# Row maxima of an attention kernel: one shared 120-row stack against own 64-row stacks, two heads side by side in TensorE

## The chip, the cores and the metric

One core of one Trainium2 chip runs the whole kernel. The metric is the device time of one execution in microseconds (us), the median of several runs. Engines are named as the profile names them: PE is TensorE's matmuls and PEld its weight loads, DVE is VectorE, ACT is ScalarE, POOL is GpSimd, SP is SyncE, which issues most DMAs.

## The reference

A transformer block on x of shape 8 x 1024 x 256: attention with 16 heads of 16, a gated relative position bias, then a layer norm, then a mixture of 8 experts (top 2, with a capacity and a fallback) and a second layer norm. The part that the change touches is the softmax:

```python
q, k, v = split_heads(x @ Wq.T + bq), ...            # 8 x 16 x 1024 x 16
gate_out = gate_a * (gate_b * gru_const - 1.0) + 2.0  # one per batch, head, query
gated_bias = gate_out * pos_bias[None]                # pos_bias depends on key - query
scores = einsum('bhid,bhjd->bhij', q, k) / sqrt(16) + gated_bias
attn = softmax(scores, axis=-1)
```

The bias differs from key to key only near the diagonal; beyond 192 positions it is one constant for each side.

## The kernel before

**Two passes over the scores.** The exponentials are computed with keys in the partitions and queries along the row, so a row's maximum can't be subtracted there. A first pass, "the maxima", therefore computes scores with queries in the partitions, takes the maximum of each row, and stores it, negated, as two more rows of the stacked queries (`shift`). The second pass (`scores`, `exps`) then gets shifted scores out of its matmul.

**Stacks.** q and k are split into three bf16 parts each. A float product is approximated by six products of parts (`PRODUCTS`), and these are stacked in the contraction dimension: 6 x 16 = 96 rows, 24 rows for the constant far bias, 2 for the shift. `QS` and `KS` hold these 122 rows for the two heads of a unit; `KD` holds the same stack (120 rows) for the differences of keys. `load_unit` (L901) fills the stacks of a unit by DMAs from DRAM, 16 rows of each head at a time, all on SyncE's queue.

**The maxima.** The 128 keys of a block are taken as two halves of 64. max(first, second) = second + relu(first - second), so one bank gets the difference of the halves (a=1, keys from `KD`) and one the second half (a=0, from `KS`). Each is one "far" matmul of the 120-row stack with 512 columns (L1023) and one "near" matmul that adds the bias by a diagonal of gates, `dgb` (L1027, `half_scores`). `max_first` (L1037) does a=1 into bank pm1 and lets ScalarE write relu of it to `over`; `max_second` (L1054) does a=0 into pm0, or into the bank that is shared by the other work; `max_fold` (L1060) lets VectorE add both and take the maximum in the next step.

**Order of the work.** The order is written out by hand and each engine runs its list in that order. A unit is two heads of a batch: 64 units of 16 steps. Step s of unit u does one block of keys j and one half c of the queries: `scores` (L1102, two matmuls), `exps` (L1115: VectorE adds the near bias, ScalarE takes exp), and every second step (c=1) `products` with v (L1132: eight matmuls in 32-column parts of the array). In the same step the maxima of step m = g + 21 are done, so they run 21 steps ahead (`LEAD`), one head at a time. Projections, gates, output projection and routing of neighbouring batches are "streams" that are fed in between, at most one bank task a step (`streams.bank`); `held` lets the reader of the bank run in the next step.

**PSUM.** Two score tiles of two banks each, pm0 and pm1, one bank for everything else, one for the products.

**SyncE's list within a unit.** The sums of the outputs (s=2, after ScalarE has copied the products), the loads of `KS`, `KD` (s=3, 4), the sums' return (s=5), `QS` (s=6) of unit u+2, the bias of u+1 (s=8), its gates (s=9 and 15), the divided outputs and the row maxima (s=11, 12).

The lead and the loop over steps:

```python
for m in range(LEAD):
    if m:
        max_fold(m - 1)
    ...
    streams.held()
    max_first(m)
    streams.free()
    streams.bank()
    max_second(m)
```

After attention the mixture of experts runs from about 2490 us to the end; the change doesn't touch it.

Of the kernel before, what the change touches and what calls it, by code (L numbers as in the profile page):

```python
# [21 lines left out]
P = 128  # L22
# [18 lines left out]

PRODUCTS = ((0, 0), (0, 1), (0, 2), (1, 0), (1, 1), (2, 0))
R_FAR, R_SHIFT, R_ALL = 6 * D, 6 * D + 24, 6 * D + 26
HP = 2
LEAD = 21
SHIFT_AT = -LEAD % 16
DIVIDE_AT = 10
EPS = 1e-5

# [29 lines left out]
def tile_attention_moe(  # L79
# [73 lines left out]
    with ExitStack() as at:  # L153
# [210 lines left out]
        for t in fd:  # L364
# [3 lines left out]
            nc.sync.dma_start(  # L368
                out=flat, in_=zero16.unsqueeze(1).to_broadcast([P, flat.shape[1], 2 * E])
            )  # L370
        QS = [cst.tile([R_ALL, HP, N], BF16, name=f"qs{i}") for i in range(3)]
        KS = [cst.tile([R_ALL, HP, N], BF16, name=f"ks{i}") for i in range(3)]
        KD = [cst.tile([R_SHIFT, HP, N // 2], BF16, name=f"ks_d{i}") for i in range(2)]
        pattern = once.tile([R_ALL, HP, N], F32, tag="oD", name="pattern")
        for h in range(HP):
            for part in range(3):
                r = R_FAR + part * NI
                nc.sync.dma_start(out=pattern[r : r + NI, h, :], in_=kcr[:NI, :])
            for r in range(R_SHIFT, R_ALL):
                nc.sync.dma_start(out=pattern[r : r + 1, h, :], in_=kcr[8:9, :])  # L380
        for t in KS:
            nc.gpsimd.tensor_copy(t[R_FAR:], pattern[R_FAR:])
        for t in KD:
            nc.gpsimd.memset(t[R_FAR:], 0.0)
        incl = [cst.tile([P, NE + 1, NI], F32, name=f"incl{i}") for i in range(2)]
        prefix = [cst.tile([P, 2 * NI], F32, name=f"prefix{i}") for i in range(3)]
        for t in prefix:
# [513 lines left out]
        def load_unit(u, which):  # L901

            b, hp = divmod(u, UB)
            assert batches[b].gated and batches[b].rows >= (hp + 1) * HP * D
            heads = slice(hp * HP * D, (hp + 1) * HP * D)
            if which == 2:
                nc.sync.dma_start(
                    out=QS[u % 3][R_FAR:R_SHIFT],
                    in_=fd[b % 2][:, :, hp * HP : (hp + 1) * HP, :].rearrange(
                        "a j h n -> (a j) h n"  # L910
                    ),
                )
            src, dst = ((kd, KS[u % 3]), (dd, KD[u % 2]), (qd, QS[u % 3]))[which]
            for r, parts in enumerate(PRODUCTS):
                nc.sync.dma_start(
                    out=dst[r * D : (r + 1) * D],
                    in_=src[b % 2][parts[which != 2], heads, :].rearrange(
                        "(h d) n -> d h n", d=D
                    ),
                )  # L920

        def load_max_bias(u):

# [86 lines left out]

        def half_scores(m, a, pm):
            u, n = divmod(m, STEPS)
            i, h = divmod(n, HP)
            me = units[u]
            lo, hi = max(i - NEAR, 0), min(i + NEAR + 1, NI)
            pm = pm.rearrange("p (j n) -> p j n", n=HALF)
            if a:
                keys = KD[u % 2][:, h, :].rearrange("p (j n) -> p j n", n=HALF)  # L1020
            else:
                keys = KS[u % 3][:R_SHIFT, h, :].rearrange("p (j n) -> p j n", n=P)[:, :, HALF:]
            nc.tensor.matmul(  # L1023
                pm, QS[u % 3][:R_SHIFT, h, i * P : (i + 1) * P], keys, start=True, stop=False
            )
            at = (h * 2 + a) * MWIN + (lo - i + NEAR) * P
            nc.tensor.matmul(  # L1027
                pm[:, lo:hi, :],
                dgb[m - h][:, h, :],
                me.biasb[:, at : at + (hi - lo) * P].rearrange("p (j n) -> p j n", n=P)[  # L1030
                    :, :, :HALF
                ],
                start=False,
                stop=True,
            )

        def max_first(m):  # L1037

            u, n = divmod(m, STEPS)
            me = units[u]  # L1040
            ahead = m + 6
            if m == 0:
                for a in range(0, 6, 2):
                    dgb[a] = diagonal(0, a // 2)
            if ahead % 2 == 0 and ahead < UNITS * STEPS:
                dgb[ahead] = diagonal(ahead // STEPS, ahead % STEPS // HP)
            if n == 0:
                me.mh = rt.tile([P, HP, NI], F32, tag="mh", name=f"mh{u}", bufs=2)
            me.over = rt.tile([P, CH], F32, tag="over", name="over", bufs=2)
            pm = ps_m.tile([P, CH], F32, tag="pm1", name="pm1")  # L1050
            half_scores(m, 1, pm)
            nc.scalar.activation(me.over, pm, AF.Relu)  # L1052

        def max_second(m, common=False):  # L1054

            pm = bank("pm") if common else ps_m.tile([P, CH], F32, tag="pm0", name="pm0")
            half_scores(m, 0, pm)
            units[m // STEPS].rest = pm

        def max_fold(m):  # L1060
            u, n = divmod(m, STEPS)
            i, h = divmod(n, HP)
            me = units[u]
            nc.vector.tensor_tensor_reduce(  # L1064
                out=me.over,
                in0=me.rest,
                in1=me.over,
                scale=1.0,
                scalar=-3.0e38,
                op0=ALU.add,  # L1070
                op1=ALU.max,
                accum_out=me.mh[:, h, i : i + 1],
            )

        def shift(u):
            me = units[u]
            pmr = bank("pmr")
            nc.tensor.transpose(
                pmr[: HP * NI, :P], me.mh.rearrange("p h i -> p (h i)"), ident
            )  # L1080
            yield HELD
            rows = rt.tile([HP * NI, 2, P], BF16, tag="row", name=f"row{u}", bufs=2)
            nc.scalar.mul(rows[:, 0, :], pmr[: HP * NI, :P], -1.0)
            yield SLOW
            nc.vector.scalar_tensor_tensor(
                rows[:, 1, :], pmr[: HP * NI, :P], -1.0, rows[:, 0, :],
                ALU.mult, ALU.subtract,
            )

            def store():  # L1090
                for a in range(2):
                    nc.sync.dma_start(
                        out=QS[u % 3][R_SHIFT + a : R_SHIFT + a + 1].rearrange(
                            "o h (i q) -> o (h i) q", q=P
                        ),
                        in_=rows[:, a, :],
                    )

            after(1, store)


        def scores(u, j, c):  # L1102
            me = units[u]
            qs, ks = QS[u % 3], KS[u % 3]
            me.sc = ps_s.tile([P, HP, CH], F32, tag="sc", name=f"sc{u}_{j}")
            for h in range(HP):
                nc.tensor.matmul(  # L1107
                    me.sc[:, h, :],
                    ks[:, h, j * P : (j + 1) * P],
                    qs[:, h, c * CH : (c + 1) * CH],  # L1110
                    start=True,
                    stop=True,
                )
# [148 lines left out]
            streams.step()  # L1262
        clear = clearing()
        for u in range(2):
            for which in range(3):
                load_unit(u, which)
            load_max_bias(u)
            clear_max_bias(u)
# [3 lines left out]
        for m in range(LEAD):  # L1272
            if m:
                max_fold(m - 1)
            if m == STEPS:
                streams.drain()
                streams.own.append(shift(0))
            streams.held()
            max_first(m)
            streams.free()  # L1280
            streams.bank()
            max_second(m)
        streams.drain()
        for j in range(2):
            gate_biases(0, j)
# [23 lines left out]
        for g in range(G + 12):  # L1309
# [4 lines left out]
            if g < G:  # L1314
# [5 lines left out]
                if sb == 60:  # L1320
                    streams.start(rows(b))
                if u + 2 < UNITS:
                    for which, at_ in enumerate((3, 4, 6)):
                        if s == at_:
                            load_unit(u + 2, which)
                    if s == 1:
# [1 line left out]
                    if s == 7:  # L1328
                        clear_max_bias(u + 2)
                if u + 1 < UNITS:  # L1330
                    if s == 8:
                        load_bias(u + 1)
                    for which, at_ in enumerate((9, 15)):
# [4 lines left out]
            streams.held()  # L1338
            if g < G:
                scores(u, j, c)  # L1340
                if m < G:
                    max_first(m)
                exps(u, j, c)
            streams.free(c == 1)
            if c == 1 and 1 < g < G + NCH:
                pu, pj = (u, j - 1) if j else (u - 1, NI - 1)
                products(pu, pj, prs)
            if c == 1 and g < G:
                prs = units[u].pr
            if u and s == DIVIDE_AT:  # L1350
                streams.own.append(divide(u - 1))
            if s == SHIFT_AT and u + 1 < UNITS:
# [1 line left out]

            behind = c == 0 and streams.read == SLOW
            others = s + 1 != SHIFT_AT
            if not behind:
                streams.bank(others)
            if m < G and g < G:
                max_second(m, c == 0 and not behind and not streams.holder)  # L1360
            if behind:
                streams.bank(others)
            if g < G and c == 0:
                gu, gj = divmod(g // 2 + 2, NI)
                if gu < UNITS:
# [270 lines left out]
```

## Time and profile before

| | |
|---|---|
| median of 3 runs | 3673.83 us (3670.74 to 3685.23) |
| the profiled execution | 3676.38 us, span 3674.6 us |
| granted TensorE clock, mean | 0.961 |
| PE busy | 3285.5 us, 89% |
| DVE, ACT, POOL busy | 1930.6, 2045.6, 2223.5 us |
| far matmuls, a=1 and a=0 (L1023) | 392.9 and 396.1 us, 1024 each |
| near matmuls (L1027) | 577.9 us, 2048 |
| scores (L1107), products (L1137) | 619.3 us (2048), 553.9 us (4096) |
| exp (ACT L1129) | 1047.4 us, 1024 |

In a row of the profile's groups the first number after the bar is the busy time in us, the next the mean length of one in ns; behind the second bar stands the engine's idle time just before, and what ended most of it. Matmuls overlap: one with 512 columns is shown as 0.38 us long, while the next can start 0.22 us after it. In the timeline a row has its start, its length, the engine, line and operation, the tiles, and in brackets the idle time before it with the releaser. "x8" are eight merged into one row.

### The profile page before, as it was taken

What the parts mean: (1) busy time and instruction counts of PE and PEld (TensorE: products, weight loads), DVE (VectorE), ACT (ScalarE), POOL (GpSimd) and SP (SyncE); (2) the same over time, 40 slices, a digit from 0 to 9 for tenths busy, and PEclk for the clock granted to TensorE, in tenths of its full rate; (3) what the DMA queues carried; (4) which work ended last, traced back from release to release, by engine and by line L of the source; (5) the groups of instructions that cost most, each with busy time, mean ns of one, the idle gap of its engine ahead of it and who ended that gap; (6) DMA issues with size and microseconds to landing.
All of it is one profiled execution on the core that took longest, in us unless ns stands there. A gap on an engine that the chain in (4) does not pass through costs nothing. (4 is left out here: it accounts for less than half of the span.)

```text
span 3674.6 us, 53450 instructions
## 1 busy us (share of the span) xinstructions
PE 3285.5 (89%) x16263; PEld 1656.9 (45%) x16263; DVE 1930.6 (53%) x5559; ACT 2045.6 (56%) x3084; POOL 2223.5 (61%) x2619
## 2 busy tenths in 40 slices
PE   4698999989999999999999999984399999999998
PEld 2243343333334334334334433332267677667776
DVE  2455656655665665665666576651134344444443
ACT  1577777767777777777787777871022222222222
POOL 2566666876887887787787788782233333333332
PEclk8899999999999999999999999996699999999999
DMA  5567666656553444444434444330332322223220
GB/s 130 150 169 200 171 182 182 186 172 185 169 154 112 150 140 128 126 136 126 141 121 148 129 135 130 123 102 14 110 86 59 88 89 56 91 93 94 73 90 21
DMA packets 380593, 455.70 MB, mean 124 GB/s; under 512 B 87653, under 2 KB 285410, under 8 KB 380282
## 3 DMA queue, kind: packets, MB, share of 16 engines
q1 hardware_dynamic: 338602, 388.06, 35.6%
q0 software_dynamic: 19296, 43.38, 4.2%
q10 hardware_dynamic: 22384, 20.58, 1.9%
q8 instruction: 138, 2.26, 0.3%
q14 instruction: 173, 1.42, 0.1%
HBM read 315.16 MB, written 140.54 MB: 124 GB/s over the span
## 5 line engine op out<-in xcount | busy, mean ns | idle before, releaser
L1129 ACT ACTIVATE pr<-sc 128x1024 f32<-128x1024 f32 x1024 | 1047.4, 1024 | 332.2 <-DVE sc L1122 328.8
L983 POOL TENSOR_TENSOR gb<-bias,gates 128x1024 f32<-128x1024 f32 (+2 forms) x512 | 1071.5, 2093 | 178.0 <-DMA gates<-gd 102.6
L1064 DVE CUSTOM_DVE_ANT_0 over<-pm,over 128x512 f32<-128x512 f32 x1024 | 703.7, 687 | 815.0 <-ACT over L1052 302.4
L1052 ACT ACTIVATE over<-pm 128x512 f32<-128x512 f32 x1024 | 611.3, 597 | 280.4 <-PE pm L1027 264.6
L1107 PE MATMUL sc<-qs,ks 122*128 122x512 bf16 x2048 | 619.3, 383 | 42.8 <-ACT pr L1129 32.5
L1122 DVE TENSOR_TENSOR sc<-sc,gb 128x640 f32<-128x640 f32 (+3 forms) x768 | 599.7, 781 | 94.2 <-POOL gb L983 80.9
L1027 PE MATMUL pm<-biasb,dgb 128*128 128x320 bf16 (+2 forms) x2048 | 577.9, 282 | 16.7 <-POOL dgb L996 16.7
L1137 PE MATMUL o_acc<-pr,v 128*17 128x512 f32 x4096 | 553.9, 612 | 0.3 <-ACT pr L1129 0.3
L1474 PE MATMUL ph<-xsT,w 128*128 128x512 f32 (+1 forms) x1440 | 488.6, 497 | 13.0 <-ACT xsT L1414 13.0
L1489 PE MATMUL py<-w,hT 128*128 128x256 f32 x2208 | 485.0, 379 | 6.5 <-DVE ys L1496 6.5
L1489 PEld LDWEIGHTS py<-w,hT 128*128 128x128 f32 x2208 | 419.2, 190 | 75.2 <-issue 9.8
L1023 PE MATMUL pm<-ks,qs 120*128 120x512 bf16 x1024 | 396.1, 387 | 43.8 <-DVE mh L1064 25.1
L1023 PEld LDWEIGHTS <-qs 120*128 120x128 bf16 x2048 | 207.3, 101 | 502.6 <-issue 334.7
L1023 PE MATMUL pm<-ks_d,qs 120*128 120x512 bf16 x1024 | 392.9, 384 | 39.2 <-DMA qs<-qd 25.7
L1481 ACT ACTIVATE hT<-ph,b_sb 128x512 f32<-128x512 f32 (+1 forms) x360 | 211.6, 588 | 288.3 <-PE ph L1474 284.7
L1474 PEld LDWEIGHTS ph<-xsT,w 128*128 128x128 f32 x1440 | 270.7, 190 | 213.3 <-issue 167.3
L1414 ACT COPY xsT<-pt 128x512 f32<-128x512 f32 (+1 forms) x90 | 39.5, 489 | 568.6 <-PE pt L1411 473.8
L143 POOL TENSOR_TENSOR rs<-rstd,neghalf 128x1 f32<-128x1 f32 x138 | 78.3, 567 | 438.4 <-DVE rstd L141 437.5
L1027 PEld LDWEIGHTS <-dgb 128*128 128x128 bf16 x2048 | 201.7, 98 | 278.9 <-issue 147.5
L996 POOL TENSOR_TENSOR dgb<-anti,grev 128x256 bf16<-128x256 f32 x512 | 315.1, 616 | 4.9
L1107 PEld LDWEIGHTS <-ks 122*128 122x128 bf16 x2048 | 197.9, 99 | 227.8 <-issue 82.6
L1509 POOL DMA_INDIRECT out_dram<-o,dst_i x138 | 145.3, 1053 | 158.1 <-DVE o L145 69.5
(184 smaller groups left out, 2861.2 us busy)
## 6 DMA issues: line engine op xcount, KB each, us to landing
gates<-gd SPq DMA_DIRECT2D x64, 832.0 KB
biasb<-stripb SPq DMA_DIRECT2D x128, 288.0 KB
gates<-gd SPq DMA_DIRECT2D x64, 576.0 KB
bias<-blocks SPq DMA_DIRECT2D x64, 512.0 KB
xd<-zero SPq DMA_DIRECT2D x51, 522.0 KB
ks<-kd SPq DMA_DIRECT2D x384, 64.0 KB
qs<-qd SPq DMA_DIRECT2D x384, 64.0 KB
yd<-zero SPq DMA_DIRECT2D x40, 512.0 KB
```

The costliest lines, as they stand in the source:

```text
L983: nc.gpsimd.tensor_tensor(gb_[:, :, off : off + hi - lo], me.bias[:, :, off : off + hi - lo], gates[:, :, lo - at : hi - at], ALU.mult,)
L996: nc.gpsimd.tensor_tensor(dg, anti.unsqueeze(1).to_broadcast([P, HP, P]), batches[b].grev[:, i, hp * HP : (hp + 1) * HP] .unsqueeze(2) .to ...
L1023: nc.tensor.matmul(pm, QS[u % 3][:R_SHIFT, h, i * P : (i + 1) * P], keys, start=True, stop=False)
L1027: nc.tensor.matmul(pm[:, lo:hi, :], dgb[m - h][:, h, :], me.biasb[:, at : at + (hi - lo) * P].rearrange("p (j n) -> p j n", n=P)[:, :, :HALF],
L1052: nc.scalar.activation(me.over, pm, AF.Relu)
L1064: nc.vector.tensor_tensor_reduce(out=me.over, in0=me.rest, in1=me.over, scale=1.0, scalar=-3.0e38, op0=ALU.add, op1=ALU.max, accum_out=me. ...
L1107: nc.tensor.matmul(me.sc[:, h, :], ks[:, h, j * P : (j + 1) * P], qs[:, h, c * CH : (c + 1) * CH], start=True, stop=True,)
L1122: nc.vector.tensor_tensor(sc[:, :, lo - c * CH : hi - c * CH], sc[:, :, lo - c * CH : hi - c * CH], me.gb[j][:, :, off : off + hi - lo], A ...
L1129: nc.scalar.activation(pr, sc, AF.Exp)
L1137: nc.tensor.matmul(o_acc[r : r + D + 1, :], batches[b].v[:, j, hp * HP + h, :], prs[c][:, h, :], start=(j == 0), stop=(j == NI - 1),)
L1474: nc.tensor.matmul(ph[:, :size], w1_sb[:, k, f * P : (f + 1) * P], xsT[:, k, :size], start=(k == 0), stop=(k == NK - 1),)
L1489: nc.tensor.matmul(py, hT[:, f, t * P : (t + 1) * P], w2_sb[:, f, :], start=(f == 0), stop=(f == NF - 1),)
```

## The change

The maxima get stacks of their own. `QM` and `KM` hold, for each head, 64 rows: three products of parts (`M_PRODUCTS`: q0k0, q0k1, q1k0) of 16 rows each, and 16 rows of the far bias in two parts. Head 0 lies in partitions 0 to 63, head 1 in 64 to 127. A step's far matmuls are now those of both heads for one a, each over its 64 rows of the array, into pm0 and pm1; an even step does a=1, the odd one a=0. Thus a pair of steps does what two steps did before. The two Relus come together in the even step, the two folds together at the start of the next even step. `KM` also gets the second halves of the keys as a copy of its own, so that `KS` and `QS` are needed only by the exponentials: two buffers, loaded for u+1 at s=3 and 6. `KM` and `QM` are loaded for u+2 at s=4 and 7. The maxima run 22 steps ahead. In even steps a bank task comes ahead of the maxima unless VectorE is reading one in that step; `streams.free` moves to the step's end. The shared bank is no longer used for maxima.

```diff
+M_PRODUCTS = PRODUCTS[:2] + PRODUCTS[3:4]
+M_FAR = 3 * D
-LEAD = 21
-SHIFT_AT = -LEAD % 16
+LEAD = 22
+SHIFT_AT = -LEAD % 16 + 1
...
+        QS = [cst.tile([R_ALL, HP, N], BF16, name=f"qs{i}") for i in range(2)]
+        KS = [cst.tile([R_ALL, HP, N], BF16, name=f"ks{i}") for i in range(2)]
+        QM = [cst.tile([P, N], BF16, name=f"qm{i}") for i in range(2)]
+        KM = [cst.tile([P, 2, N // 2], BF16, name=f"km{i}") for i in range(2)]
...
+            if which == 0:
+                for r, (_, part) in enumerate(PRODUCTS):
+                    rows(KS[u % 2], r * D, kd, part)
+            elif which == 1:
+                nc.sync.dma_start(
+                    out=QS[u % 2][R_FAR:R_SHIFT],
...
+                for r, (part, _) in enumerate(PRODUCTS):
+                    rows(QS[u % 2], r * D, qd, part)
+            else:
+                for h in range(HP):
+                    head = slice((hp * HP + h) * D, (hp * HP + h + 1) * D)
+                    if which == 3:
+                        nc.sync.dma_start(
+                            out=QM[u % 2][64 * h + M_FAR : 64 * (h + 1)],
...
+                    for r, (qpart, kpart) in enumerate(M_PRODUCTS):
+                        to = slice(64 * h + r * D, 64 * h + (r + 1) * D)
+                        if which == 3:
+                            nc.sync.dma_start(
+                                out=QM[u % 2][to, :], in_=qd[b % 2][qpart, head, :]
+                            )
+                        else:
+                            nc.sync.dma_start(
+                                out=KM[u % 2][to, 0, :].rearrange("d (j n) -> d j n", n=HALF),
...
+                            nc.sync.dma_start(
+                                out=KM[u % 2][to, 1, :], in_=dd[b % 2][kpart, head, :]
+                            )
...
+        def half_scores(m, a):
...
+            pms = [ps_m.tile([P, CH], F32, tag=f"pm{h}", name=f"pm{h}") for h in range(HP)]
+            for h, pm in enumerate(pms):
+                rows = slice(64 * h, 64 * (h + 1))
+                nc.tensor.matmul(
+                    pm, QM[u % 2][rows, i * P : (i + 1) * P], KM[u % 2][rows, a, :],
+                    start=True, stop=False,
+                )
+            for h, pm in enumerate(pms):
...
+                nc.tensor.matmul(
+                    pm.rearrange("p (j n) -> p j n", n=HALF)[:, lo:hi, :],
+                    dgb[m - n % HP][:, h, :],
...
+        def maxima(m):
+            u, n = divmod(m, STEPS)
+            me = units[u]
+            if n % HP:
+                me.rest = half_scores(m, 0)
+                return
...
+            me.over = []
+            for pm in half_scores(m, 1):
+                over = rt.tile([P, CH], F32, tag="over", name="over", bufs=3)
+                nc.scalar.activation(over, pm, AF.Relu)
+                me.over.append(over)
...
         def max_fold(m):
             u, n = divmod(m, STEPS)
+            if n % HP == 0:
+                return
...
+            for h in range(HP):
+                nc.vector.tensor_tensor_reduce(
...
         for u in range(2):
-            for which in range(3):
+            for which in ((2, 3, 0, 1), (2, 3))[u]:
                 load_unit(u, which)
...
                 if u + 2 < UNITS:
-                    for which, at_ in enumerate((3, 4, 6)):
+                    for which, at_ in ((2, 4), (3, 7)):
...
                 if u + 1 < UNITS:
+                    for which, at_ in ((0, 3), (1, 6)):
...
+            if c == 0 and not behind:
+                streams.bank(others)
+            if m < G and g < G:
+                maxima(m)
+            if g < G:
                 exps(u, j, c)
             if c == 1 and 1 < g < G + NCH:
                 pu, pj = (u, j - 1) if j else (u - 1, NI - 1)
                 products(pu, pj, prs)
...
+            if c == 1 or behind:
                 streams.bank(others)
+            streams.free(c == 1)
```

## The prediction, before the run

> **What bounds the kernel now.** I read the busy time of the engines in stretches first, then TensorE's waits, then the timeline of single pairs of steps, last SyncE's queue. The attention stage runs from about 149 to 2490 us: 1024 steps, 512 pairs, 2341/512 = 4.57 us a pair. One stretch of it (columns: stretch, length, then busy us of PE, PEld, DVE, ACT, POOL):
>
> ```profile
> 1470.00:1654.00 184.00, 172.17 (x959) 67.06 (x959) 118.81 (x290) 138.79 (x199) 145.76 (x191) 0.99 0.44 131
> ```
>
> PE is busy for 94%, no other engine over 80%. TensorE is the bound here, and its waits say how near the others are (us in total, times, longest):
>
> ```profile
> PE sc L1107 <- ACT pr L1129: 32.5, 29, 3.5
> ...
> PE pm L1023 <- DMA qs<-qd: 25.8, 18, 8.2
> PE pm L1023 <- DVE mh L1064: 25.1, 51, 1.7
> ...
> PE pm L1023 <- ACT over L1052: 8.4, 23, 0.9
> ```
>
> The last three are the waits of the maxima: for rows from DRAM and for their two banks. They are small today, 59 us together, and the change rebuilds all three. The reader should keep the readers' durations at hand:
>
> ```profile
> L1064 DVE CUSTOM_DVE_ANT_0 over<-pm,over 128x512 f32<-128x512 f32 x1024 | 703.7, 687 | 815.0 <-ACT over L1052 302.4
> L1052 ACT ACTIVATE over<-pm 128x512 f32<-128x512 f32 x1024 | 611.3, 597 | 280.4 <-PE pm L1027 264.6
> ```
>
> **Matmul by matmul.** A "far" matmul (L1023) is the stacked 120-row product, a "near" one (L1027) the bias. Starts are what counts, since a matmul's row is longer than its slot:
>
> ```profile
> 1903.17 0.27 PE L1027 MATMUL pm<-biasb,dgb 128*128 128x256 bf16 x1
> ...
> 1903.38 1.05 PE L1137 MATMUL o_acc<-pr,v 128*17 128x512 f32 x8
> ...
> 1904.36 0.39 PE L1023 MATMUL pm<-ks,qs 120*128 120x512 bf16 x1
> ...
> 1904.59 0.27 PE L1027 MATMUL pm<-biasb,dgb 128*128 128x256 bf16 x1
> ...
> 1904.70 0.59 PE L1107 MATMUL sc<-qs,ks 122*128 122x512 bf16 x2
> ```
>
> Near to next takes 0.11 us (1904.59 to 1904.70), but 0.21 us ahead of the products (1903.17 to 1903.38), which use 32-column parts of the array. The eight product matmuls take 0.98 us: two waves of four side by side at 0.43 us each, and 0.12 us to leave. The division's matmul uses four rows of the array, so it is the nearest row to the change's 64-row matmuls:
>
> ```profile
> 1627.17 0.25 PE L1027 MATMUL pm<-biasb,dgb 128*128 128x192 bf16 x1
> ...
> 1627.26 0.59 PE L1107 MATMUL sc<-qs,ks 122*128 122x512 bf16 x2
> ...
> 1627.91 0.25 PE L1027 MATMUL pm<-biasb,dgb 128*128 128x192 bf16 x1
> ...
> 1628.08 1.12 PE L1177 MATMUL pb<-recs,sel 4*128 4x512 f32 x2
> ```
>
> Again 0.17 in place of 0.09 us. So a switch of the array's shape costs about 0.09 us each way, in columns and in rows.
>
> **Part 1, the far matmuls side by side.** Before, four a pair at 0.218 = 0.87 us. After, each step has one group of two: 0.09 to enter, 0.01 of weight load that is no longer hidden, 0.02 between the two starts (the four products start within 0.02), 0.215, and 0.10 to leave = 0.44 us; two groups a pair are 0.88 us. The Trainium skill, "TensorE: Matmul & The Clock Gate", Part 3 (measured speedup), lets matmuls in distinct row groups share a slot with about 4 ns between starts; by that alone a pair saves 2 x 0.21 = 0.42 us, 215 us in 512 pairs. "TensorEngine Tiling (Array Packing)", Key Properties, speaks against it: a change of tiling mode drains TensorE. The row of the four-row matmul sides with the second, and each step enters and leaves. Bounds: gain of 0.39 us a pair (no drain for 64 rows), loss of 0.16 (the second weight load not hidden, 0.1 us by its row). I take 0, by the nearest row.
>
> **Part 2, the banks.** Before, pm1 carries the a=1 half (read by ScalarE) and pm0 or the spare bank the a=0 half (read by VectorE), each once a step, so a reader has a step to free its bank. After, both banks are filled in the even step, both read by ScalarE, both filled again in the odd step. Count from the even step's first near matmul. It ends at 0.285 (mean row). The Relu starts 0.04 later (the usual distance in the trace), the second 0.48 later (ScalarE's spacing), and ends 0.60 after that: 1.40, and TensorE sees it at 1.45. TensorE meanwhile does two near matmuls (0.24), scores (0.43) and the entry with its offset (0.12) = 0.79. It then stands 0.66 us at the second far matmul of the odd step; queued behind are the near matmuls, the products and the next scores. The mode switch of the odd step is hidden in this wait, its exit isn't. The other half of the ring: near at 0, fold starts 0.285 + 0.15, second fold 0.62 later, its end with the accumulator's read 0.70, TensorE 0.05: 1.81 us. Beside it lie 0.24 + 0.09 + 0.98 + 0.43 + 0.10 = 1.84 us: no wait, but no slack either if VectorE has other work.
> The 0.66 us is covered only where a stream's bank work comes between the two maxima, which the new order does only when VectorE read a stream's bank in the even step. All bank work is some 460 tasks; I take it that a quarter of the pairs is covered: 0.75 x 0.66 = 0.50 us x 512 = 253 us. Of today's waits those for the exp (32.5), the fold (25.1) and the Relu (8.4) go, as their place is taken: 253 - 66 = **+187 us**. Bounds: 0 (all covered) to 338 (none).
>
> **Part 3, SyncE's queue.** One unit, in light load (start, length of all, count at the end; the last line is TensorE's):
>
> ```profile
> 1614.82 2.45 SPq L1154 DMA_DIRECT2D sums<-osb  x4
> 1617.37 2.86 SPq L915 DMA_DIRECT2D ks<-kd  x6
> 1620.27 2.78 SPq L915 DMA_DIRECT2D ks_d<-dd  x6
> 1623.15 2.45 SPq L1164 DMA_DIRECT2D recs<-sums  x4
> 1625.65 0.55 SPq L907 DMA_DIRECT2D qs<-fd  x1
> 1626.24 2.67 SPq L915 DMA_DIRECT2D qs<-qd  x6
> ```
> ```profile
> 1631.26 0.38 PE L1023 MATMUL pm<-ks_d,qs 120*128 120x512 bf16 x1 [1.21 <-DMA qs<-qd]
> ```
>
> SyncE waits for the unit's outputs (L1154), then issues without a pause, 0.465 us each, up to the query rows of unit u+2; they land about 1.9 us after the last issue ends, and the first maxima of u+2 (s=11) already wait 1.2 us. The change makes 33 issues of these 19: KM 12 for KD's 6, QM 8 more. QM comes last, behind KS, KM, sums' return and QS. That is 14 x 0.465 = 6.5 us later, and the maxima start one step earlier (s=10). KM and QM have new forms (16 rows each, pieces of 128 B): between 0.42 and 0.60 us by the rows of other small issues, so 6 to 10 us; I take 6.5. From the issue of sums, by means over units as the trace shows them:
> - 25 units under 34 us: the last issue ends at 14.8, ready at 14.8 + 6.5 + 1.9 = 23.2; s=10 would want it at 14.3, plus 4.5 pairs of Part 2's 0.5 = 16.6. Wait 6.6 us: 165 us.
> - 15 units of 34 to 40 us: 15.4 and 17.0, unit by unit a mean wait of 4.5: 68 us.
> - 22 units over 40 us: 16.6 and 22.0, mean 1.45: 32 us.
>
> Together **+265 us** (393 if Part 2 costs nothing, since then the maxima want the rows sooner; near 0 if SyncE ran ahead of its wait). Behind the waiting matmul stands all of TensorE; ScalarE runs dry after two score tiles. Behind QM on SyncE stand the bias, the gates and the divided outputs; they move by the same 6.5 us, but the steps that want them are moved by the stall, so nothing is added.
>
> **Part 4, the clock.** The records grant half clock for 3.4 us after 3.8 us of idle TensorE (296.6 to 300.4). 38 units would wait over 3.4 us. A full window of lost half is 1.7 us, part of it falls in waits; I take 1.0: **+38 us** (0 to 65).
>
> **Part 5, the start.** GpSimd's clearing of the max-bias tiles, with the first diagonals behind it, waits for loads that stand behind the first units' rows; these become 53 issues where there were 38: 15 x 0.465 = 7 us. The lead's 22 steps run without scores at the ring's 4.4 us a pair (48 us) where 21 took 37 (111.4 to 148.8). The new patterns cost some small setup. Together **+18 us**, 5 to 30.
>
> **At nothing:** two buffers of QS and KS (their last reader is done before s=3), a third `over`, the streams' work moved to the end of the step (same order on SyncE), the larger traffic (DMA share 0.44).
>
> Sum: 187 + 265 + 38 + 18 = 508 us on the profiled execution's 3676.4, which lies 2.5 above the median 3673.8: 4182, say 4180.
>
> **Rivals.**
> 1. As above: bank ring and SyncE's chain both bind. 4180. Chance 0.55.
> 2. The loads come in time (SyncE's issues are cheaper, or land sooner than I count), the ring binds: 3674 + 187 + 18 = 3880. For it: units over 40 us have 5 us to spare today. Against: the light units wait already. 0.2.
> 3. The Relus are hidden (bank work lies between the halves oftener), the chain binds: 3674 + 393 + 38 + 18 = 4125. 0.1.
> 4. The two far matmuls don't run side by side, or every stall gets a slow clock and late folds on top: 0.2 x 512 = 100 us and more, 4300. For it: nothing in the trace shows 64-row groups together. 0.08.
> 5. Faster, one mechanism: 64-row groups switch without a drain, so a pair sheds 0.39 us of TensorE, and the Relus' wait, read ahead by streams, stays under that. It decides as soon as the mean wait is below 0.39 us and QM is no later than s=10. At half of the 0.66: (0.33 - 0.39) x 512 = -31 us, 3643. Against: both conditions fail in the rows above. 0.07, of which 0.03 stays within 0.5%, about what a measurement of this kernel can tell from no change.
>
> Faster 0.04, same 0.03, slower 0.93. The range 3840 to 4320 takes in rivals 2 and 3 and most of 4.
>
> **What would show it.** Relu to far waits (PE pm on ACT over) rising from 8 to some 200 us, on every odd step; PE pm waiting on DMA for QM about once a unit, 250 us in all; SyncE's run of issues at about 22 us a unit; far pairs starting within 0.1 us with 0.09 us lost on either side; PE's busy share falling to about 80% in the stage. It would be wrong if the starts around the far pairs show no lost 0.09, if SyncE has gaps between sums and QM, or if TensorE's wait for the Relus is under 0.3 us a pair.

## The result and the profile after

The changed kernel takes 4235.1 us (median of 4 runs, 4224.5 to 4248.5) against 3672.3 us for the kernel before on the same chip: ratio 1.153, 95% interval 1.150 to 1.156. It is slower by 15%; the forecast was 4180 us in a range of 3840 to 4320.

The page's groups of the changed kernel answer to those shown of before (after the first bar: busy us, mean ns; after the second: the engine's idle time ahead):

```profile
L1109 ACT ACTIVATE over<-pm 128x512 f32<-128x512 f32 x1024 | 556.5, 595 | 1054.8 <-PE pm L1080 1050.5
L1074 PE MATMUL pm<-km,qm 64*128 64x512 bf16 x2048 | 626.7, 406 | 385.9 <-DMA qm<-qd 203.5
L1119 DVE CUSTOM_DVE_ANT_0 over<-pm,over 128x512 f32<-128x512 f32 x1024 | 666.2, 688 | 358.8 <-PE pm L1080 320.3
L1080 PE MATMUL pm<-biasb,dgb 128*128 128x320 bf16 (+2 forms) x2048 | 437.0, 298 | 23.7 <-DMA gates<-gd 23.7
```

The readers cost what they cost before (595 and 688 ns against 597 and 687); ScalarE and VectorE only stand longer. The far matmuls' busy time fell from 789 to 627 us, and yet TensorE now stands 386 us just ahead of them. Its waits (us in total, times, longest) name the new one:

```profile
PE pm L1074 <- DMA qm<-qd: 203.5, 94, 7.9
...
PE pm L1074 <- DMA qm<-fd: 55.3, 14, 6.4
PE pb L1232 <- DMA recs<-sums: 50.2, 23, 8.3
...
PE pm L1074 <- ACT over L1109: 16.4, 72, 0.9
```

259 us for the query rows of the maxima, and 50 us for the returned sums. The last line must not be read as "the Relus cost 16 us". The timeline of one pair of steps shows why:

```profile
1879.62 0.60 PE L1162 MATMUL sc<-qs,ks 122*128 122x512 bf16 x2
...
1880.15 0.39 PE L1074 MATMUL pm<-km,qm 64*128 64x512 bf16 x2
...
1880.48 0.45 PE L1080 MATMUL pm<-biasb,dgb 128*128 128x320 bf16 x2
...
1880.76 0.60 PE L1162 MATMUL sc<-qs,ks 122*128 122x512 bf16 x2
1880.82 1.09 ACT L1109 ACTIVATE over<-pm 128x512 f32<-128x512 f32 x2 [1.09 <-PE pm L1080]
...
1881.47 0.86 PE L1074 MATMUL pm<-km,qm 64*128 64x512 bf16 x2
...
1882.27 0.45 PE L1080 MATMUL pm<-biasb,dgb 128*128 128x320 bf16 x2
...
1882.64 1.05 PE L1192 MATMUL o_acc<-pr,v 128*17 128x512 f32 x8
```

The even step's two far matmuls (1880.15) are one row of 0.39 us: they do run side by side. The odd step's (1881.47) are one row of 0.86 us: the first waited for one Relu, the second for the other, which ended at 1881.91. The profile puts much of this wait down to the weight loads as "issue", so the rows by releaser hide it. Here are those rows of the far matmuls' weight loads, the changed kernel's first, then that of the kernel before; they hold other idle time of PEld too:

```profile
PEld L1074 <- issue: 674.2, 1081, 8.5
```
```profile
PEld L1023 <- issue: 334.7, 443, 8.9
```

Starts show the wait itself: from the scores' second matmul to the second far one it is 315 ns (median) in even steps, 983 in odd ones.

A table of my own from the starts of the scores' matmuls: the time of a pair of steps by its place in the unit, mean of units 2 to 61.

| pair of steps (s) | 0,1 | 2,3 | 4,5 | 6,7 | 8,9 | 10,11 | 12,13 | 14,15 | unit |
|---|---|---|---|---|---|---|---|---|---|
| before | 4.46 | 4.88 | 4.76 | 4.22 | 4.29 | 5.66 | 3.99 | 4.74 | 37.0 |
| after | 4.77 | 4.96 | 5.07 | 4.50 | 4.88 | 12.04 | 4.40 | 5.25 | 45.9 |

Seven pairs grew by 0.08 to 0.59 us, 0.354 in the mean; the pair at s=10, where the maxima of unit u+2 start, grew by 6.38. With the eighth pair's 0.354 taken out of it, that is 6.03 x 62 = 374 us at the one place and 0.354 x 8 x 62 = 175 us in all pairs; the stage starts 26 us later (174.5 against 148.8). Together that is 575 us where the span grew by 565 (the means of 60 units stand for all); the rest of the kernel is the same within 3 us. SyncE's list in a unit that was light before shows the place:

```profile
1884.37 2.44 SPq L1209 DMA_DIRECT2D sums<-osb  x4
1886.92 2.86 SPq L930 DMA_DIRECT2D ks<-kd  x6
1889.82 0.57 SPq L964 DMA_DIRECT2D km<-kd  x1
1890.43 0.58 SPq L970 DMA_DIRECT2D km<-dd  x1
...
1897.79 2.45 SPq L1219 DMA_DIRECT2D recs<-sums  x4
1900.28 0.55 SPq L939 DMA_DIRECT2D qs<-fd  x1
1900.87 2.89 SPq L930 DMA_DIRECT2D qs<-qd  x6
...
1906.12 1.34 SPq L960 DMA_DIRECT2D qm<-qd  x3
```

and TensorE at the end of it:

```profile
1907.19 0.58 PE L1074 MATMUL pm<-km,qm 64*128 64x512 bf16 x1 [4.61 <-DMA qm<-fd]
...
1908.99 0.58 PE L1074 MATMUL pm<-km,qm 64*128 64x512 bf16 x1 [1.22 <-DMA qm<-qd]
...
1911.96 1.91 PE L1192 MATMUL o_acc<-pr,v 128*17 128x512 f32 x8
```

From sums to the last query row SyncE issues for 23.1 us without a pause. Then TensorE runs at half clock for a while: the records grant 0.5 from 1904.8 to 1915.1 us, and the eight products take 1.91 us where they took 1.05 (at 1882.64).

### The profile page after: what moved, and what is told of

It is laid out like the page before. It is cut to its first block, busy times and chain, and to the rows that moved or that the text cites. A ratio compares the mean times of both kernels' runs of the same rounds, so it can differ in the third digit from the quotient of the medians.

```text
span 4239.3 us, 54221 instructions
## 1 busy us (share of the span) xinstructions
PE 3558.2 (84%) x16263; PEld 1542.5 (36%) x16263; DVE 1961.1 (46%) x5559; ACT 2015.8 (48%) x3084; POOL 2225.6 (52%) x2626
## 5 line engine op out<-in xcount | busy, mean ns | idle before, releaser
L1109 ACT ACTIVATE over<-pm 128x512 f32<-128x512 f32 x1024 | 556.5, 595 | 1054.8 <-PE pm L1080 1050.5
L1184 ACT ACTIVATE pr<-sc 128x1024 f32<-128x1024 f32 x1024 | 1017.7, 1037 | 67.9 <-DVE sc L1177 67.3
L1074 PE MATMUL pm<-km,qm 64*128 64x512 bf16 x2048 | 626.7, 406 | 385.9 <-DMA qm<-qd 203.5
L1119 DVE CUSTOM_DVE_ANT_0 over<-pm,over 128x512 f32<-128x512 f32 x1024 | 666.2, 688 | 358.8 <-PE pm L1080 320.3
L1162 PE MATMUL sc<-qs,ks 122*128 122x512 bf16 x2048 | 651.9, 401 | 8.5 <-ACT pr L1184 6.4
L1192 PE MATMUL o_acc<-pr,v 128*17 128x512 f32 x4096 | 586.2, 646 | 0.3 <-ACT pr L1184 0.3
L1080 PE MATMUL pm<-biasb,dgb 128*128 128x320 bf16 (+2 forms) x2048 | 437.0, 298 | 23.7 <-DMA gates<-gd 23.7
L1074 PEld LDWEIGHTS <-qm 64*128 64x128 bf16 x2048 | 144.3, 93 | 828.0 <-issue 674.2
L1080 PEld LDWEIGHTS <-dgb 128*128 128x128 bf16 x2048 | 118.5, 99 | 505.2 <-issue 463.0
L441 POOL TENSOR_TENSOR parts<-rest,parts 128x512 bf16<-128x512 f32 (+1 forms) x80 | 92.3, 1154 | 301.9 <-ACT parts L440 297.9
```

Of the source, the lines that this page charges most:

```text
L1074: nc.tensor.matmul(pm, QM[u % 2][rows, i * P : (i + 1) * P], KM[u % 2][rows, a, :], start=True, stop=False,)
L1080: nc.tensor.matmul(pm.rearrange("p (j n) -> p j n", n=HALF)[:, lo:hi, :], dgb[m - n % HP][:, h, :], me.biasb[:, at : at + (hi - lo) * P].r ...
L1109: nc.scalar.activation(over, pm, AF.Relu)
L1119: nc.vector.tensor_tensor_reduce(out=me.over[h], in0=me.rest[h], in1=me.over[h], scale=1.0, scalar=-3.0e38, op0=ALU.add, op1=ALU.max, accu ...
L1162: nc.tensor.matmul(me.sc[:, h, :], ks[:, h, j * P : (j + 1) * P], qs[:, h, c * CH : (c + 1) * CH], start=True, stop=True,)
L1184: nc.scalar.activation(pr, sc, AF.Exp)
```

## The experiments

All ratios are to the kernel before, on the same chip, with a 95% interval. The runs were made on several chips, on which the kernel before took 3672 to 3690 us, so where two of the new kernels are compared the ratios are safer than the microseconds. Pairs of steps are those of the table above, taken from each run's trace in the same way.

**e1: the loads early.** KM and QM of u+2 ahead of the sums.

```diff
-                    for which, at_ in ((2, 4), (3, 7)):
+                    for which, at_ in ((2, 0), (3, 1)):
```

> The changed kernel with KM and QM of unit u+2 issued at s=0 and 1, ahead of the sums of the outputs, instead of s=4 and 7. Theory (bank ring and SyncE's chain, about half each): TensorE's waits for QM, 259 us in the changed kernel's profile, fall under 30 us, and some 40 us of half clock go with them: about 3940 us (3900 to 3990), and the 0.67 us at each odd step's second far matmul stays. Rival (the ring, or the array's switches, are all of the loss): the waits for QM are only where the ring's time shows, and the time stays above 4150.

3911.8 us, 1.062 (1.061 to 1.064): 323 us less than the changed kernel (333 by the ratios). The pair at s=10 falls from 12.04 to 4.96 us, 7.08 x 62 = 439 us. The odd step's wait stays (981 ns against 983), and so do the pairs at s=2, 4, 12 and 14, within 0.1 us. So SyncE's chain, and the half clock after it, are over half of the loss (half clock is granted for 160 us of the stage, not some 530), and the ring is another part, as the theory said. But the pair at s=6 rose from 4.50 to 6.32, 1.82 x 62 = 113 us:

```profile
PE pm L1074 <- DVE mh L1119: 74.6, 80, 4.7
```
```profile
DVE sums L1225 <- DMA ks<-kd: 91.5, 31, 5.1
...
DVE sums L1225 <- DMA sums<-osb: 74.0, 23, 7.8
```

The sums now come late, VectorE stands for them at its reciprocal, and the folds are queued behind it. (The first of the two rows names the load that SyncE issues just behind the sums; the reciprocal reads only the sums.)

**e2: the same matmuls over all rows, one after the other.** KM is loaded as before; each head's QM is a tile of 128 rows with zeros in the other head's (`over` has two buffers for room, as also in e7, e11 and e12).

```diff
-                    pm, QM[u % 2][rows, i * P : (i + 1) * P], KM[u % 2][rows, a, :],
+                    pm, QM[u % 2][:, h, i * P : (i + 1) * P], KM[u % 2][:, a, :],
```

> The changed kernel with the two far matmuls of a step over all 128 rows of the array, one after the other: the weights of each head have zeros in the other head's rows, so the array never changes its shape for them. Theory (what two heads side by side save, the two switches take): the far matmuls take 0.43 us a step against 0.44, and the time is that of the changed kernel within 25 us, 4210 to 4260. Rival A (switching the array is a main cost): about 200 us faster, 4030. Rival B (side by side really saves 0.2 us a step): up to 200 us slower, 4430.

4209.5 us, 1.144 (1.142 to 1.146): 25 us, 0.8% by the ratios, faster than the changed kernel and half a microsecond under the range. Side by side gains nothing over one after the other. In the odd step the second far matmul starts 980 ns after the scores, as it did (983): it stands for its bank, whatever the shape.

**e7: e1 and e2 together.**

> The early loads of e1 together with e2's far matmuls over all 128 rows. Theory (switches take what side by side saves; where the odd step stands for the second Relu, the exit of 0.1 us is paid with nothing saved): 0.1 us x 512 pairs faster than e1: 3850 to 3900. Rival (side by side saves TensorE time once the loads no longer bind): slower than e1, 3950 to 4100.

3880.7 us, 1.051 (1.049 to 1.053), by the ratios 1.1% less than e1. From the scores to the products the odd step takes 1.78 us against 1.88 in e1 (medians), and the quickest tenth of the pairs at s=2 3.90 against 4.00: that is the 0.1 us of the exit in the odd step. e2 and e7 both reject the rival that side by side saves time.

**e3: the second Relu on VectorE.**

```diff
+                if me.over:
+                    nc.vector.tensor_scalar(over, pm, 0.0, None, ALU.max)
+                else:
                     nc.scalar.activation(over, pm, AF.Relu)
```

> The changed kernel with the second Relu of a pair on VectorE instead of behind the first one on ScalarE. Theory (TensorE waits in the odd step for the second Relu): that wait falls from 0.67 to about 0.45 us, 0.2 us x 500 pairs; in the steps ahead of QM's arrival the wait for QM takes it back, so 45 to 100 us faster: 4135 to 4190. Rival (the wait is not the Relu's, but the scores' exp or the fold): no change or slower, 4230 and more.

4261.9 us, 1.158 (1.156 to 1.160): a miss, no gain. The second far matmul of the odd step did start earlier (725 ns after the scores, not 983), so the time is the rival's, but not for its reason. I took the loss to be VectorE's queue behind QM, and e6 tried that.

**e6: e1 and e3 together.**

> The early loads of e1 together with e3's second Relu on VectorE. Theory (e3's gain of 0.26 us at the far matmul was lost because VectorE, queued behind a Relu whose maxima wait for QM, held up everything behind it): without the waits for QM the gain shows, about 0.2 us x 400 pairs: 3912 - 80 = 3830. Rival (VectorE's own work ahead of the folds takes it back in any case): 3900 or more.

3996.9 us, 1.084 (1.081 to 1.087): 85 us (2.1% by the ratios) slower than e1, so that guess was wrong. The exp's wait, first in e1 and then in e6, tells where it goes:

```profile
ACT pr L1184 <- DVE sc L1177: 126.0, 94, 6.0
```
```profile
ACT pr L1187 <- DVE sc L1180: 580.1, 590, 6.1
```

The Relu stands in VectorE's list ahead of the bias of the same step's scores and waits there for the maxima. The bias, and with it the exp, come late. The pairs at s=2 and 4 are 0.3 us longer than in e1, and the pair at s=6, where VectorE stands for the sums, 0.76. That the late bias is the cause is read from these waits; no run takes it away alone.

**e4: only the issues, in the kernel before.** 14 loads of 16 rows into a spare tile, between KD and the sums' return.

```diff
+                    if s == 4:
+                        ub, uhp = divmod(u + 2, UB)
+                        for r in range(14):
+                            nc.sync.dma_start(
+                                out=spare[r // 2 * D : (r // 2 + 1) * D, r % 2, :],
+                                in_=qd[ub % 2][0, uhp * HP * D : uhp * HP * D + D, : N // 4],
+                            )
```

> The kernel before with 14 more small loads on SyncE's queue in each unit (16 rows of 512 B into a tile that nobody reads), between KD's and the return of the sums. Only the issue time of the change is added. Theory (SyncE's serial issue decides when the maxima's rows arrive): the wait for QS grows from 26 us to about 240, plus 30 us of half clock: 3910 us (3850 to 3980). Rival (the issues are hidden, SyncE has time): under 3700.

3995.7 us, 1.085 (1.084 to 1.087), 316 us more than before. The pair at s=10 went from 5.66 to 10.79 us: 5.1 x 62 = 318. (Of the others, s=14 grew by 0.53, and s=2 and 4 together shrank by as much.) So the place is the theory's, while the loss is larger than the 235 us or so that were expected and outside the range, and the first waiter is another:

```profile
PE pb L1178 <- DMA recs<-sums: 188.9, 40, 8.3
...
PE pm L1024 <- DMA qs<-qd: 51.8, 35, 8.3
```

The division (s=10) stands for the sums' return, which is behind the same 14 issues, and QS only for the rest. The two rows hold 241 us (38 before). The records grant half clock for some 480 us of the stage, 85 before; how much of the loss that makes was not separated.

**e5: the kernel before with its loads early.**

```diff
-                    for which, at_ in enumerate((3, 4, 6)):
+                    for which, at_ in enumerate((1, 0, 2)):
```

> The kernel before with its own loads of u+2 ahead of the sums: KD at s=0, KS at s=1, QS at s=2, instead of 4, 3 and 6. Theory (SyncE's chain is already just binding in the kernel before): the waits for QS, 26 us, and some half clock go: 3630 to 3665 us. Rival (SyncE has slack before the change): no change, within 10 us of 3676.

3854.0 us, 1.044 (1.041 to 1.046): a clear miss. The pair at s=10 gained 0.7 us, the pairs at s=4 and 6 lost 1.5 and 2.6: VectorE's reciprocal waits 243 us in all for sums (57 times). Here the loads cost more ahead of the sums than behind them.

**e8: e1, with the even step's bank task after the maxima.**

```diff
+            if m < G and g < G:
+                maxima(m)
             if c == 0 and not behind:
                 streams.bank(others)
-            if m < G and g < G:
-                maxima(m)
```

> The early loads of e1, and the even step's bank task always after the maxima, so that it lies in the wait for the two Relus. About 158 of 501 even steps have such a task ahead of the maxima in the changed kernel. Theory (a pair costs the ring's time, bank work in the Relu window is free): up to 0.6 us x 158 = 95 us faster than e1: 3820 to 3870. Rival (the fold's half of the ring then binds in these pairs and takes it back): within 25 us of 3912.

3904.9 us, 1.057 (1.055 to 1.060): by the ratios 0.5% less than e1, a fifth of what the theory allowed and within the rival's 25 us. Four pairs, at s=2, 8, 10 and 14, are 0.29 to 0.36 us shorter; the pair at s=6, where VectorE stands for the sums, is 1.05 longer. So bank work in the Relu window is worth about a third of a microsecond in the mean of such a pair, and what takes it back lies in one pair and not, as the rival had it, in each of them. In that pair the reciprocal waits longer for the sums (242 us in all against 166 in e1); why the sums come later wasn't settled.

**e9: the loads where SyncE has time.** KM of u+3 at s=13, QM of u+2 at s=6, ahead of QS.

```diff
-                    for which, at_ in ((2, 4), (3, 7)):
-                        if s == at_:
-                            load_unit(u + 2, which)
+                    if s == 6:
+                        load_unit(u + 2, 3)
...
+                if u + 3 < UNITS and s == 13:
+                    load_unit(u + 3, 2)
```

> The changed kernel with its loads where SyncE has time and nothing waits behind them: KM of unit u+3 at s=13 of unit u, QM of u+2 at s=6 ahead of QS, so that sums and their return aren't held up as in e1. Theory (in e1 the sums came late, VectorE's reciprocal stood for them, and the folds behind it let TensorE wait 75 us): e1's 3912 - 60 to 90 us: 3820 to 3860. Rival (all of SyncE's loss was already gone in e1): 3890 to 3930.

4062.3 us, 1.104 (1.101 to 1.106): a miss. The pairs at s=6 and 10 are short now (4.49 and 4.91), but the row maxima's store is issued after the load of s=13. Its 12 issues stand ahead, and the next unit's scores wait for it; the pairs at s=14 and 0 take 8.48 and 5.79 us:

```profile
PE sc L1162 <- DMA qs<-row: 183.1, 53, 8.3
```

**e12: head by head.** The loads of e9, the full rows of e2, and the order far, near, far, near.

```diff
-            for h, pm in enumerate(pms):
-                rows = slice(64 * h, 64 * (h + 1))
-                nc.tensor.matmul(
...
+            for h in (1, 0) if spare else (0, 1):
+                far(h)
+                close(h)
```

> The loads of e9, the far matmuls over all 128 rows as in e2, and in each step head 0's far and near matmul, then head 1's, instead of both far ones first; the two banks and the pair of steps stay. Theory (putting both heads side by side makes both banks' readers start late: the first Relu could start 0.2 us sooner, and TensorE needs its bank back 0.3 us later): the odd step's wait falls from 0.63 to about 0.2 us: 0.4 x 512 = 200 us faster than e9 with full rows (about 3800): 3620 to 3720. Rival (the pair's ring takes its time in whatever order): within 30 us of 3800.

3999.2 us, 1.086 (1.084 to 1.087). The total missed, for e9's reason, which I had not seen when I wrote the expectation:

```profile
PE sc L1173 <- DMA qs<-row: 276.2, 57, 9.6
```

The step that it was for came out. In the six pairs from s=2 to 13, which that wait doesn't touch, e9 takes 28.6 us and e12 26.1: 0.41 us a pair. The 0.4 of the forecast was meant against e9 with full rows, and full rows alone are worth about 0.1 of it (e2 and e7), so some 0.3 belong to the order. The unit's six pairs are also shorter than in the kernel before (27.8), whose pair at s=10 holds a wait for QS; without that wait (e10 below) they take 27.1. The odd step, scores first:

```profile
1901.26 0.60 PE L1173 MATMUL sc<-qs,ks 122*128 122x512 bf16 x2
1901.75 0.38 PE L1080 MATMUL pm<-km,qm 128*128 128x512 bf16 x1
1901.97 0.30 PE L1087 MATMUL pm<-biasb,dgb 128*128 128x320 bf16 x1
...
1902.24 0.38 PE L1080 MATMUL pm<-km,qm 128*128 128x512 bf16 x1
1902.45 0.30 PE L1087 MATMUL pm<-biasb,dgb 128*128 128x320 bf16 x1
1902.68 0.62 PE L1203 MATMUL o_acc<-pr,v 128*17 128x512 f32 x4
```

Scores to products are 1.42 us, where the changed kernel took 1.88 (1880.76 to 1882.64 above) and full rows without the new order 1.78 (e7): head 0's work fills head 1's wait.

**e11: e12 with a third bank.** Where no stream wants the shared bank, head 1's second half goes there, and first.

```diff
-            spare = False
+            spare = a == 0 and common
```

> e12 (the next one), and in odd steps in which no stream waits for the shared bank, head 1's second half goes into that bank and is done first, so that it needn't wait for a Relu. Theory (the ring of two banks is the rest of the loss): some 0.2 us less in perhaps half of the pairs than e12, 20 to 50 us: 3620 to 3690. Rival (no bank is short any more): as e12.

4002.3 us, 1.086 (1.085 to 1.088), as e12. Five of the six pairs are about 0.1 us shorter, the pair at s=10 is 0.5 longer, and the unit comes to 42.0 against 42.1 us. With head by head, the two banks are no longer what a third one could relieve by much; what lengthens the pair at s=10 wasn't looked into.

**e10: the kernel before, KD for u+3 at s=13.** The sums stay first, QS is issued sooner.

```diff
-                    for which, at_ in enumerate((3, 4, 6)):
+                    for which, at_ in ((0, 3), (2, 6)):
...
+                if u + 3 < UNITS and s == 13:
+                    load_unit(u + 3, 1)
```

> The kernel before with KD loaded for u+3 at s=13 instead of for u+2 at s=4, so that QS is issued 2.8 us sooner after the sums, which stay where they are. Theory (SyncE's chain is just binding before, and e5 lost only by holding up the sums): the waits for QS, 26 us, go: 20 to 40 us faster than the kernel before, ratio 0.990 to 0.995. Rival: no change.

3658.4 us, 0.993 (0.992 to 0.995): 0.7% faster than the kernel before, as forecast. Its wait for QS is gone from the list; the scores wait 36 us for the row maxima's store (7 before), and the pair at s=14 is 0.59 us longer, so the same slip as in e9 costs it a part.

## Why the prediction was right

**The direction and the place.** Both named mechanisms bind: e1 removes the chain and leaves the ring, e12 shortens the ring's wait by its order alone, and e4 puts the chain's issues into the kernel before.

**Part 1 (far matmuls, taken as 0).** Right. In even steps the two start 3 ns apart (median); entering costs 0.10 us (scores to far 315 against 215 ns), leaving 0.10 (far to near 319 against 218). 0.20 is lost for 0.21 saved, and e2 puts the net at nothing gained. Of the two rules that the prediction set against each other, both hold in this trace: the matmuls of two row groups do share a slot (the Trainium skill, "TensorE: Matmul & The Clock Gate", Part 3, measured speedup), and the change of tiling mode is paid ("TensorEngine Tiling (Array Packing)", Key Properties). With one slot saved at a time the second cancels the first.

**Part 2 (bank ring, +187).** The wait was given as 0.66 us; the median is 983 - 315 = 0.67. That a quarter of the pairs is covered was wrong: the mean over the odd steps with the scores just ahead is 0.63, so hardly any are, and 512 pairs of it are 322 us. The net is 175 us all the same. The 66 us of today's waits that were to go weren't the reason: their three rows still hold 36 us. But the kernel before had waits at its banks that the rows of its waits name only in part. A quiet pair of it, at s=2:

```profile
1255.05 0.69 DVE L1064 CUSTOM_DVE_ANT_0 over<-pm,over 128x512 f32<-128x512 f32 x1 [1.83 <-ACT over L1052]
...
1255.40 0.30 PE L1027 MATMUL pm<-biasb,dgb 128*128 128x320 bf16 x1
...
1255.66 0.08 DVE L1064 DVE_READ_ACCUMULATOR2_ANT mh<- 128x1 f32 x1
...
1255.80 0.38 PE L1023 MATMUL pm<-ks,qs 120*128 120x512 bf16 x1
```

The far matmul comes 0.40 us after the near one, just after VectorE's fold has left the bank at 1255.74; where nothing holds it, it comes after 0.14. The change takes this 0.26 us away: in the quickest tenth of the pairs at s=2, 3.63 us became 4.00, which is 0.37 = 0.63 - 0.26. Over the whole stage the far matmuls of the kernel before stood an estimated 95 us (each start less the shortest after the same kind of matmul, without the waits for QS), where the prediction had 34. With 26 us that the exp's row lost, this is most of the 147 us between 322 and 175; the rest wasn't traced. So the total was right by two errors that cancel, which is luck. What was to show it, the row of PE pm on ACT over at some 200 us, failed too: it shows 16.4, since the wait lies mostly with the weight loads.

**Parts 3 and 4 (SyncE's chain +265, clock +38).** The mechanism is right, the size too low: 374 us at the place of the wait against 303. The mis-sized term is the price of KM's issues, put at 0.465 us. They take 0.61 each (1889.82 and 1890.43 are two starts), and the run from sums to the last load grew by 8.2 us (15.64 to 23.88 in the mean), not 6.5, though inside the 6 to 10 that were allowed. Some 59 units of 62 wait for these rows, and 1.7 us in each is about 100 us. Against it stands that the far matmul starts 1.5 us after the last issue ends (median), where 1.9 were counted: 24 us less. Together that is near the 71 us that are missing. TensorE's waits for QM, 259 us, came near the 265; to them come 50 us at the sums' return, which I had not charged, and half clock. The records grant it for some 530 us of the stage after, 85 before; how much of that is lost and not idle anyway wasn't separated.

**Part 5 (start, +18).** 26 us.

**Rivals.** 2 and 3 each hold one part alone, and e1 shows that both are there. The first half of 4 fell with the 3 ns; its other half, that stalls bring a slow clock, is in part true, as the 530 us show. 5 fell with both its conditions: the mean wait is 0.63 us and not under 0.39, and QM comes late. PE's share fell to 84% in the stretch from 1800 to 2000 us (167.3 of 200), not quite the 80 given.

Left open: the order of e12 with KM's load after the row maxima's store. Its six undisturbed pairs are 0.9 us a unit below those of e10, the better of the two with the old stacks, but it was not run.

## What to carry to other kernels

An engine's gain from smaller tiles has to be set against what opens and closes them, and against the readers: two banks filled together are freed late, one after the other, and head by head the same matmuls take some 0.3 us less a pair. Count the issues of a DMA queue as serial work with a place in the order; the price of 14 more is what stands behind them (316 us here, with nothing else changed). A load that is moved forward makes something behind it late: each of the four placements tried here (e1, e5, e9, e10) did so. Three still gained on balance, and in e5 it cost more than the old wait. And a wait that no row names has to be looked for in the starts: both kernels had one at their banks.

## What the runs showed of the hardware

Two 64-row matmuls into two banks start 3 ns apart when both banks are free, and each change between 64 rows and the full array costs 0.10 us (315 against 215 ns going in, 319 against 218 coming out); the four-row matmul of the kernel before had told about 0.09. KM's loads (16 rows in 128-byte pieces and 16 rows of 1 KB, in turn) go out every 0.61 us from SyncE, QM's 16 rows of 2 KB and the 32-row ones of the kernel before every 0.47; what makes the difference wasn't tried. And around the one stall followed here, 4.61 and 1.22 us of TensorE's waiting up to 1909.0, the granted clock was 0.5 from 1904.8 to 1915.1, so the matmuls behind it ran at about half speed (1.91 against 1.05 us for the same eight).
